# Sending the generated weights of a tile row to DRAM in two stages: four tap columns, then three

## The chip, the cores and the metric

The kernel runs on one core of a Trainium2 chip. The metric is device time in microseconds (us), given as the median of repeated runs. A profile of one execution stands beside it: its span is the time from the first to the last instruction.

## What is computed

Two layers over a batch of 32 images of 256 channels and 32 x 32 pixels. Each begins with a group normalization (`_gn`, 32 groups) and adds its result to its input.

```python
# layer 0: a 3x3 convolution in fp16 (values clamped), 256 -> 256 channels
x = x + _L0_conv_ref(_gn(x), L0_conv_weight, L0_conv_bias)
# layer 1: an involution, whose 7x7 kernels are generated at each pixel
y = jnp.einsum('oc,bchw->bohw', w1, x)                  # 256 -> 64
y = relu(y * scale + shift)                             # batch norm
w = jnp.einsum('oc,bchw->bohw', w2, y) + b2             # 64 -> 16 groups * 49 taps
w = w.reshape(b, G, K * K, H, W)
patches = ...                                           # 7x7 neighbourhood of each pixel
out = jnp.einsum('bgkhw,bgckhw->bgchw', w, patches)     # 16 groups of 16 channels
```

The x of the second part stands for the normalized input of layer 1. The weights w differ from pixel to pixel: 16 x 49 values at each of 1024 pixels of each image.

## The kernel before

**The work of one image.** `front(b)` does everything up to the generated features: group normalization, the convolution (line 332, tile `pc`), the second normalization, the features `y_sb`, and the transposed pixels. `weights(b, r0)` turns the features of four image rows (a chunk, WR = 4) into involution weights: TensorE multiplies into `pw` (line 410), and VectorE adds the bias and writes the result into `w_sb` (line 428).

`w_sb` is a ring of 24 image rows. The 7 tap columns dj lie in it by `divmod(dj, 2)`: the quotient picks one of four blocks of 32 partitions (one partition for each image column), the remainder e picks one of two planes. So even tap columns lie in plane e = 0 and odd ones in plane e = 1, and each is written by VectorE adds of its own.

**The way through DRAM.** The involution is done as matrix products against banded weights, and the layout needed for that is made by writing to DRAM and reading back:

- `scatter(b, k)` (line 477) writes the weights of tile row k (8 image rows, 4 tile rows an image) from `w_sb` to the DRAM tensor `wd`: one DMA of 160 KB for each of the 7 tap columns, all issued by SyncE (called SP in the profile).
- `load_bands(b, k)` (line 490) reads the tile row from `wd` into one of three band buffers: 16 DMAs of 70.2 KB, of which 14 are issued by GpSimd (POOL) and two by SyncE. All seven tap columns have to be in `wd` by then.
- `sums(b, m)` (line 515) multiplies pixels and bands on TensorE into `acc`, half a tile row at a time. `add_windows(b, m)` (line 531) adds `acc` to the image on VectorE.
- `store(b, k)` (line 536) writes half an image to the output and `load_x` (line 105) loads an image as two halves. Both are issued by SyncE, at 512 KB for each DMA.

**The order.** The order of instructions on each engine is written out by hand: a loop over steps n, 16 to an image. `due(n, lag)` says which image and which step i of that image a kind of work belongs to in step n. An engine executes its own instructions in this order and waits only where data or a buffer requires it, so a step is a place in each engine's queue and not a time. Within one step the order is: `front`, `sums`, `add_windows`, `store`, `weights`, `scatter`, `load_x`, `load_bands`.

With LEAD = 18, a chunk of weights is made in each even step. The scatter of a tile row is in the step after the last chunk that it needs. Counted modulo 16, the scatters of tile rows 0, 1, 2 and 3 fall into steps 3, 7, 11 and 13. The loads of bands fall into steps 3 (tile row 3 of the image before), 7 (tile row 0), 11 (tile row 1) and 15 (tile row 2). The stores fall into steps 12 (first half) and 15 (second half), and the load of an image into step 1. The bands of a tile row are loaded nine steps before its sums.

Of the kernel before, what the change touches and what calls it, by code (L numbers as in the profile page):

```python
# [14 lines left out]
B, C, H, W = 32, 256, 32, 32  # L15
# [5 lines left out]
K1, PAD1 = 7, 3  # L21
# [18 lines left out]
TR = RG * XR  # L40
SIDES = 2
JC = W // SIDES
K = H // TR
# [17 lines left out]
WR = 4  # L61
# [6 lines left out]
LEAD = 18  # L68
# [3 lines left out]
def tile_quant_conv_then_involution(  # L72
# [29 lines left out]
    def load_x(b):  # L102
        xt = xpool.tile([P, CH, N], F32, tag="x", name=f"x_{b}")
        for h in range(CH):
            nc.sync.dma_start(xt[:, h], x[b, h * P : (h + 1) * P])
        return xt
# [91 lines left out]
    def quantize_weights():  # L198

        for kh in range(CH):  # L200
            nc.vector.tensor_scalar(wq[:, kh], staged[kh], F16_MAX, -F16_MAX, ALU.min, ALU.max)
            nc.gpsimd.memset(bands[kh], 0.0)
        nc.gpsimd.memset(w_sb, 0.0)
# [198 lines left out]
    def weights(b, r0):  # L402

        pws = [ps_w.tile([P, 2, 2, SW], F32, tag=f"pw{i}", name=f"pw{i}") for i in range(2)]
        for r in range(2):
            for t in range(T):
                for i in range(2):
                    half = slice(i * CR, (i + 1) * CR)
                    dj = slice(2 * t, min(2 * t + 2, K1))
                    nc.tensor.matmul(  # L410
                        pws[i][t * TW : (t + 1) * TW, r, : dj.stop - dj.start],
                        y_sb[b % 2][half, (r0 // 2 + r) * W : (r0 // 2 + r + 1) * W],
                        w2_sb[half, dj],
                        start=True,
                        stop=True,
                    )
        for i in range(2):
            for e in range(2):
                p = P if e == 0 else (K1 // 2) * TW
                for r, rows, d0, d1, at in ring_pieces(b, r0 + 2 * i):  # L420

                    to = w_sb[:p, e]
                    to = bass.AP(
                        tensor=to.tensor,
                        offset=to.offset + at * WB + K1 - 1 - d0,
                        ap=[to.ap[0], [WB, rows], [WB - 1, d1 - d0], [WIN, G]],
                    )
                    nc.vector.tensor_tensor(  # L428
                        to,
                        pws[i][:p, r : r + rows, e, d0 * G : d1 * G].rearrange("p r (d g) -> p r d g", g=G),  # L430
                        b2_sb[:p, e, d0 * G : d1 * G]
                        .unsqueeze(1)
                        .to_broadcast([p, rows, (d1 - d0) * G])
                        .rearrange("p r (d g) -> p r d g", g=G),
                        ALU.add,
                    )
# [26 lines left out]
                    d += 1  # L463
        return pieces

    def scatter(b, k):

        at = (b * H + k * TR) % RING
        for dj in range(K1):
            t, e = divmod(dj, 2)  # L470
            to = bass.AP(
                tensor=wd.tensor,
                offset=wd.offset + k * TR * ROW + dj * WPIX + (K1 - 1 - dj) * WB,
                ap=[[WPIX, TW], [ROW, TR], [1, WB]],
            )
            rows = w_sb[t * TW : (t + 1) * TW, e, at : at + TR]
            nc.sync.dma_start(to, rows.rearrange("p s g r -> p s (g r)"))  # L477

    def load_bands(b, k):

        band = bands[(b * K + k) % NBAND]
        for i in range(JC):
            j = i // 2 + i % 2 * JC // 2
            src = bass.AP(
                tensor=wd.tensor,
                offset=wd.offset + k * TR * ROW + (j + PAD1) * WPIX,
                ap=[[ROW - 1, TR], [JC * WPIX, SIDES], [1, WPIX]],
            )
            queue = nc.sync if i % SHARE == SHARE - 1 else nc.gpsimd
            queue.dma_start(band[j::JC, :, j * WB : j * WB + WPIX], src)  # L490
# [10 lines left out]
    def sums(b, m):  # L501

        k, d = divmod(m, SIDES)
        j0 = 0 if d else PAD1
        band = bands[(b * K + k) % NBAND][:, d]
        px = pixels[(b * K + k) % NPIX][:, d]
        for h in range(CH):
            for v in range(2):
                for g, at, top, f, l in windows(b, m):
                    p = slice(g * KP, (g + 1) * KP)  # L510
                    of = band[p, g * XR + j0 * WB : g * XR + (j0 + WINI) * WB]
                    of = of.rearrange("p (j g r) -> p j g r", g=G, r=WIN)
                    for t in range(T):
                        a = h * T + t
                        nc.tensor.matmul(  # L515
                            at[t * TW : (t + 1) * TW, h, :, f - top : l - top],
                            px[p, a, v * GC : v * GC + TW],
                            of[:, :, 2 * a + v, f - top : l - top],
                            start=(h, v) == (0, 0),
                            stop=(h, v) == (CH - 1, 1),  # L520
                        )

    def add_windows(b, m):

        d = m % SIDES
        to = x_tiles[b].rearrange("p h (r c) -> p h r c", c=W)
        j0 = d * (JC - PAD1)
        for g, at, top, f, l in windows(b, m):
            x_at = to[:, :, f:l, j0 : j0 + WINI]
            of = at.rearrange("p h j r -> p h r j")[:, :, f - top : l - top]  # L530
            nc.vector.tensor_tensor(x_at, of, x_at, ALU.add)  # L531

    def store(b, k):

        cols = slice(k * NT, (k + 1) * NT)
        nc.sync.dma_start(out[b].rearrange("(h p) n -> p h n", p=P)[:, :, cols], x_tiles[b][:, :, cols])
# [5 lines left out]
    def due(n, lag):  # L542

        b, i = divmod(n - lag, per)
        return (b, i) if 0 <= b < B else (None, None)

    with tc.manual_schedule():
        fronts = {}
        for n in range(FRONT, B * per + 2):
            b, i = due(n, FRONT)  # L550
            if i == 0:
                fronts[b] = front(b)
            later = list(fronts)
            for part in range(2):
                for b in list(later):
                    got = next(fronts[b], fronts)
                    if got is fronts:
                        fronts.pop(b)
                    if got is not LATER:
                        later.remove(b)  # L560
            if n == FRONT + CH:
                quantize_weights()
            b, i = due(n, 0)
            if b is not None and i % 2 == 0:
                sums(b, i // 2)
            b, i = due(n, 1)
            if b is not None and i % 2 == 0:
                add_windows(b, i // 2)
                if i // 2 == M - 1:
                    store(b, 1)  # L570
                    x_tiles.pop(b)

            b, i = due(n, 2)
            if b is not None and i == 2 * (M - 1 - SIDES):
                store(b, 0)
            b, i = due(n, -LEAD)
            if b is not None and i % 2 == 0:
                weights(b, i // 2 * WR)

            b, i = due(n, -LEAD + 1)  # L580
            if b is not None and i % 2 == 0:
                for k in range(K):
                    if i // 2 == min((k + 1) * TR // WR, H // WR - 1):
                        scatter(b, k)
            b, i = due(n, LOAD)
            if i == 0 and b > 0:
                x_tiles[b] = load_x(b)

            b, i = due(n, 3 - 4 * NBAND)
            if b is not None and i % 4 == 0:  # L590
                load_bands(b, i // 4)
# [37 lines left out]
```

## Time and profile before

| What | Value |
|---|---|
| median of 3 runs | 1401.32 us (1395.67 to 1407.39) |
| time of the profiled execution | 1399.26 us |
| its span | 1397.5 us |
| mean granted TensorE clock | 0.979 |
| TensorE busy | 1263.0 us (90%) |
| GpSimd busy | 1009.8 us (72%) |
| VectorE busy | 926.6 us (66%) |
| ScalarE busy | 727.9 us (52%) |
| bytes moved by DMA | 369.33 MB |

Busy time is the time in which an engine executes; register, semaphore and branch instructions do not count, nor does the issue of DMAs by SyncE. GpSimd's busy time here is mostly the issue of its 1792 band loads, 548 ns each. Names such as `wd<-w_sb` say what is written and what is read. A wait is put down to what the trace saw end last before it.

### The profile page before, as it was taken

How to read it: one execution, taken by the hardware profiler on the slowest of the kernel's cores; microseconds unless marked ns; L12 is line 12 of the kernel's file. 1: busy time of each engine (PE TensorE's matmuls, PEld its weight loads, DVE VectorE, ACT ScalarE, POOL GpSimd, SP SyncE). 2: the span in 40 equal slices, each digit the busy share in tenths (PEclk: the TensorE clock that was granted, in tenths of full speed). 3: DMA queues.
4: the chain of work that ended last, by engine and by line, in shares of the span. 5: the costliest groups of instructions: out<-in, count | busy, mean ns of one | idle time of the engine just before them, and what ended most of it. 6: DMA issues, size and time to landing. Idle time of an engine off the chain costs nothing.

```text
span 1397.5 us, 70073 instructions
## 1 busy us (share of the span) xinstructions
PE 1263.0 (90%) x29440; PEld 801.1 (57%) x29440; DVE 926.6 (66%) x3179; ACT 727.9 (52%) x1699; POOL 1009.8 (72%) x1818
## 2 busy tenths in 40 slices
PE   4899999999999999998998999999999999999765
PEld 2455565556656566565655565655555655556544
DVE  3567677666776667676776666776666776777552
ACT  5865556455655546565554556463556564553200
POOL 9067777777777777778777777767776767777785
PEclk9999999999999999999999999999999999999876
DMA  6099999999999999999999999999999999999996
GB/s 215 16 248 276 253 283 289 280 274 272 286 284 274 287 278 281 278 285 274 280 287 272 272 273 282 263 278 275 273 282 267 265 282 277 282 264 269 252 257 187
DMA packets 366232, 369.33 MB, mean 264 GB/s; under 512 B 78624, under 2 KB 308192, under 8 KB 365664
## 3 DMA queue, kind: packets, MB, share of 16 engines
q1 hardware_dynamic: 279904, 235.72, 57.3%
q0 software_dynamic: 86016, 129.14, 34.7%
q8 instruction: 234, 3.83, 1.2%
q14 instruction: 78, 0.64, 0.2%
HBM read 183.81 MB, written 180.74 MB: 261 GB/s over the span
## 4 chain that ended last, share of the span: by engine, by line
PE 49%; DMA 30%; issue 6%; POOL 5%; DVE 4%; SPq 3%; ACT 2%; POOLq 0%; DVEq 0%; ACTq 0%
DMA band<-wd 23%; PE pc L332 20%; PE acc L515 15%; PE pw L410 9%; DMA wd<-w_sb 6%; POOL band L490 5%; PE py L380 3%; SPq L477 3%; DVE w_sb L428 2%; PE pt L395 2%; ACT junk L219 1%; DVE x L531 1%; DMA band<-in_w 1%; DMA x<-in_x 0%; ACT xn L278 0%
## 5 line engine op out<-in xcount | busy, mean ns | idle before, releaser
L490 POOL DMA_DIRECT2D band<-wd x1792 | 977.9, 548 | 375.4 <-DMA band<-wd 239.4
L428 DVE TENSOR_TENSOR w_sb<-pw,b_sb 128x16 f32<-128x16 f32 (+9 forms) x1920 | 454.3, 349 | 374.7 <-PE pw L410 362.0
L332 PE MATMUL pc<-xq,wq 128*128 128x496 f16 (+3 forms) x2304 | 535.1, 378 | 28.1 <-ACT xq L278 21.3
L515 PE MATMUL acc<-band,pixels 64*32 64x190 f32 (+1 forms) x16384 | 419.1, 323 | 73.8 <-DMA band<-wd 32.3
L515 PEld LDWEIGHTS acc<-band,pixels 64*32 64x32 f32 x16384 | 297.5, 108 | 165.9 <-issue 99.1
L332 PEld LDWEIGHTS <-wq 128*128 128x128 f16 x2304 | 206.5, 98 | 323.5 <-issue 110.2
L410 PE MATMUL pw<-w_sb,y 64*32 64x224 f32 (+1 forms) x8192 | 297.8, 333 | 24.1 <-issue 23.1
L531 DVE TENSOR_TENSOR x<-acc,x 128x380 f32<-128x380 f32 (+1 forms) x512 | 261.6, 511 | 35.7 <-PE acc L515 26.8
L410 PEld LDWEIGHTS pw<-w_sb,y 64*32 64x32 f32 x8192 | 183.2, 106 | 58.4 <-issue 40.6
L399 ACT COPY pixels<-pt 128x512 f32<-128x512 f32 x128 | 73.6, 575 | 234.7 <-PE pt L395 234.7
L219 ACT ACTIVATE junk<-x 128x512 f16<-128x512 f32 (+1 forms) x192 | 146.4, 763 | 14.7 <-DVE x L348 7.4
L219 ACT ACTIVATE junk<-x,mean 128x1024 f16<-128x1024 f32 x128 | 147.1, 1149 | 4.3
L250 ACT ACTIVATE s<-back,eps 128x2 f32<-128x2 f32 x64 | 18.9, 296 | 200.3 <-DVE back L235 200.2
L278 ACT ACTIVATE xn<-x,off,rstd 128x512 f32<-128x512 f32 x128 | 96.1, 800 | 0.0
L346 DVE TENSOR_SCALAR q<-pc 128x512 f16<-128x512 f32 x128 | 87.2, 681 | 12.5 <-PE pc L332 12.3
L348 DVE SCALAR_TENSOR_TENSOR x<-q,bias_sb,x 128x512 f32<-128x512 f16 x128 | 92.1, 719 | 0.2
L395 PEld LDWEIGHTS pt<-ident,xn 128*128 128x128 f32 x512 | 63.6, 142 | 27.1 <-issue 2.5
L395 PE MATMUL pt<-ident,xn 128*128 128x128 f32 x512 | 77.8, 275 | 1.2 <-ACT pixels L399 1.2
L278 ACT ACTIVATE xq<-x,off,rstd 128x1024 f16<-128x1024 f32 x64 | 76.0, 1228 | 1.4 <-PE pc L332 1.3
L240 ACT ACTIVATE mean<-back 128x2 f32<-128x2 f32 x64 | 12.7, 198 | 119.2 <-DVE back L235 119.0
L380 PEld LDWEIGHTS py<-xn,w_sb 128*64 128x64 f32 x2048 | 62.7, 138 | 16.3 <-issue 9.1
L380 PE MATMUL py<-xn,w_sb 128*64 128x64 f32 x2048 | 67.5, 224 | 2.3 <-ACT xn L278 1.8
(40 smaller groups left out, 369.5 us busy)
## 6 DMA issues: line engine op xcount, KB each, us to landing
wd<-w_sb SPq DMA_DIRECT2D x896, 160.0 KB
band<-wd POOLq DMA_DIRECT2D x1792, 70.2 KB, 5.0
x<-in_x SPq DMA_DIRECT2D x64, 512.0 KB
out<-x SPq DMA_DIRECT2D x64, 512.0 KB
band<-wd SPq DMA_DIRECT2D x256, 70.2 KB
band<-in_w SPq DMA_DIRECT2D x2, 1152.0 KB
w_sb<-in_w SPq DMA_DIRECT2D x2, 196.0 KB
wd<-band SPq DMA_DIRECT2D x2, 180.0 KB
```

Source lines behind the costliest of these rows:

```text
L219: nc.scalar.activation(junk[:, n0:n1], src[:, h, n0:n1], func, bias=bias, accum_out=self.sums[:, i : i + 1])
L278: nc.scalar.activation(dst, src, AF.Identity, bias=self.off[:, one], scale=self.rstd[:, one])
L332: nc.tensor.matmul(pc.rearrange("p (r c) -> p r c", c=W)[:, r0 - nt * RT : r1 - nt * RT, c0:c1], wq[:, kh, k, mh * P : (mh + 1) * P], xq[: ...
L346: nc.vector.tensor_scalar(q, pc, F16_MAX, -F16_MAX, ALU.min, ALU.max)
L348: nc.vector.scalar_tensor_tensor(xt[:, mh, cols], q, bias_sb[:, mh : mh + 1], xt[:, mh, cols], ALU.add, ALU.add)
L380: nc.tensor.matmul(py[i * CR : (i + 1) * CR, cols], w1_sb[:, kh, :], px[:, r : r + 2], start=kh == 0, stop=kh == CH - 1,)
L395: nc.tensor.transpose(pt[:, i, h * P : (h + 1) * P], xn[:, h, (m + i) * P : (m + i + 1) * P], ident)
L410: nc.tensor.matmul(pws[i][t * TW : (t + 1) * TW, r, : dj.stop - dj.start], y_sb[b % 2][half, (r0 // 2 + r) * W : (r0 // 2 + r + 1) * W], w ...
L428: nc.vector.tensor_tensor(to, pws[i][:p, r : r + rows, e, d0 * G : d1 * G].rearrange("p r (d g) -> p r d g", g=G), b2_sb[:p, e, d0 * G : d ...
L490: queue.dma_start(band[j::JC, :, j * WB : j * WB + WPIX], src)
L515: nc.tensor.matmul(at[t * TW : (t + 1) * TW, h, :, f - top : l - top], px[p, a, v * GC : v * GC + TW], of[:, :, 2 * a + v, f - top : l - top],
L531: nc.vector.tensor_tensor(x_at, of, x_at, ALU.add)
```

## The change

`scatter` gets an argument `part`. With part 0 it issues the tap columns 0, 2, 4 and 6, with part 1 the columns 1, 3 and 5. Part 0 stays in the step in which the whole scatter was. Part 1 is one step later, for each tile row. Within its step it stands where the scatter stands: after `store` and `weights`, ahead of `load_x` and `load_bands`.

```diff
-    def scatter(b, k):
+    def scatter(b, k, part):
 
         at = (b * H + k * TR) % RING
-        for dj in range(K1):
+        for dj in range(part, K1, 2):
             t, e = divmod(dj, 2)
...
-            b, i = due(n, -LEAD + 1)
-            if b is not None and i % 2 == 0:
-                for k in range(K):
-                    if i // 2 == min((k + 1) * TR // WR, H // WR - 1):
-                        scatter(b, k)
+            for part in range(2):
+                b, i = due(n, -LEAD + 1 + part)
+                if b is not None and i % 2 == 0:
+                    for k in range(K):
+                        if i // 2 == min((k + 1) * TR // WR, H // WR - 1):
+                            scatter(b, k, part)
             b, i = due(n, LOAD)
             if i == 0 and b > 0:
                 x_tiles[b] = load_x(b)
```

## The prediction

> **What bounds the kernel now.** I read the busy line and the slices first, then the waits, then the timelines of the two queues that issue the DMAs concerned.
>
> ```profile
> PE 1263.0 (90%) x29440; PEld 801.1 (57%) x29440; DVE 926.6 (66%) x3179; ACT 727.9 (52%) x1699; POOL 1009.8 (72%) x1818
> DMA  6099999999999999999999999999999999999996
> PE 49%; DMA 30%; issue 6%; POOL 5%; DVE 4%; SPq 3%; ACT 2%; POOLq 0%; DVEq 0%; ACTq 0%
> ```
>
> TensorE is busy in 90% of the span, and the DMA engines are above 90% in nearly every slice. The chain that ended last (third line) is half TensorE and about a third the transfers with the queues that issue them: DMA 30, POOL 5, SPq 3. So there are two near-equal bounds. Over 97 to 1350 us, the stretch without start and tail, the windows view gives TensorE 1166.4 of 1253 us, a DMA share of 0.97 and a clock of 0.99. The waits in that stretch:
>
> ```profile
> DVE w_sb L428 <- PE pw L410: 356.1, 225, 6.7
> POOL band L490 <- DMA band<-wd: 230.3, 284, 2.9
> ...
> POOL band L490 <- DMA wd<-w_sb: 19.1, 31, 2.7
> PE acc L515 <- DMA band<-wd: 18.7, 15, 2.6
> ...
> DVE w_sb L428 <- DMA wd<-w_sb: 6.6, 2, 4.2
> PE acc L515 <- DMA wd<-w_sb: 6.2, 6, 2.2
> ```
>
> Columns: total us, times, longest. GpSimd's band loads wait mainly for their own earlier landings (230.3), since eight may be outstanding: it issues in runs of about eight, 4.4 us each, then waits 1 to 2 us. TensorE loses only 18.7 + 6.2 = 25 us to transfers. The weights' way out to DRAM (wd<-w_sb) costs GpSimd at most 19.1 us and VectorE 6.6. SyncE and GpSimd around one tile row 0 (image 15):
>
> ```profile
> 673.54 1.32 SPq L105 DMA_DIRECT2D x<-in_x  x2
> 675.21 5.26 SPq L477 DMA_DIRECT2D wd<-w_sb  x7
> 680.86 1.64 SPq L490 DMA_DIRECT2D band<-wd  x2
> 682.86 5.97 SPq L477 DMA_DIRECT2D wd<-w_sb  x7
> ...
> 683.89 3.37 POOL L490 DMA_DIRECT2D band<-wd  x6
> 688.38 0.55 POOL L490 DMA_DIRECT2D band<-wd  x1 [1.13 <-DMA band<-wd]
> 689.14 3.32 POOL L490 DMA_DIRECT2D band<-wd  x6 [0.22 <-DMA wd<-w_sb]
> ```
>
> The seven taps take 5.3 us to issue, two band loads follow in 1.6 us, and GpSimd's first load of this tile row starts at 689.14. I read each landing from the semaphore updates: the last update of a DMA's semaphore before that semaphore's next DMA. Here the taps land from 681.9 to 686.8, so 689.14 stands 2.3 us after the last one.
>
> **What the skill says.** "DMA: Bandwidth & Descriptors", section "Queues, rings and completion order": every DMA engine takes turns between the queue rows, and consumes one row's ring in order. The trace agrees: the taps land in the order of issue, about 0.8 us apart, and an issue behind a 512 KB store or load lands late. The same page, "Anatomy of one DMA", prices a GpSimd DMA at about 2.0 us plus bytes/436 GB/s, which is an estimate of 2.2 us for 70.2 KB. The trace shows 2.4 at least but 5.0 in the median, so most of the landing time is sharing the engines. "Trainium Kernel Development and Optimization", "Key Constraints": DMAs of all issuers run on the same 16 engines. So moving transfers between places in a queue saves no bytes; the DMA share of 0.97 says the same.
>
> **The change, part by part.**
>
> *What moves.* All 896 taps stay, at 160 KB each. What SyncE executes is a fixed order in which it waits only for data; a step is no clock. The seven taps of a tile row were contiguous. Now taps 0, 2, 4, 6 go first and 1, 3, 5 go in the next step's place. A tile row is 10.2 us ((1368.6 - 66.3) / 127.5), a step a quarter of it, 2.6 us. Between the two stages now stand: for tile rows 0, 1 and 2, the two SyncE band loads of the tile row before (load_bands falls in the first stage's step); for row 2 also store(b, 0); for row 3 nothing. So the "stage" is worth 1.2 to 2.6 us of issue for the band loads and about 0.4 more for the store, not a full step.
>
> *Does anything hold the second stage longer?* The band loads wait for a buffer whose sums ran a step before. In the trace they start 0.1 to 1.6 us after row 0's last tap, so their data was ready. The store waits for add_windows of the step before it; behind row 2 of image 14 it issued at 660.0, right after the band loads. Each weights chunk on VectorE starts while the tile row before it is still in flight, so dependences are kept by region, and the second stage needs no later chunk. I cost extra waits at nothing, with 2 us as the upper end (the rest of a step).
>
> *When the last tap lands.* The place that tap 5 takes in the queue is today that of the second band load (rows 0, 1) or of the store (row 2). Bytes in the ring ahead of it are then the same, so I take their present landing. Against today's last tap, over images 2 to 29: row 0 +0.6 us, row 1 +1.5, row 2 +2.5 (512 KB are now ahead of it), row 3 about 0.
>
> *GpSimd.* Its first load of a tile row needs all seven taps. It starts, in the mean, 2.9, 4.4, 5.3 and 6.6 us after the last landing for rows 0 to 3; at least 0.8 of this is the pass through the waits. Subtracting 0.8 and the shifts above image by image leaves 3 of 28 rows 0 short by 1.6 us in total, one row 1 by nothing, and 3 rows 2 by 3.8: 5.4 us of new GpSimd waits. If all second stages land 1 us later still, the same sum is 19.6 us; 2 us later, 57.4. I take 8, because a 160 KB tap lands a little after a 70 KB load in the same place.
>
> *VectorE.* The ring of 24 rows in w_sb is overwritten three tile rows on. For row 0 the fifth chunk's adds come close: even taps (e = 0) have a margin of 1.3 us in the mean and 0.1 at the least, odd ones 2.4 and 1.0. The even taps now land earlier, a gain; the odd ones in the place of the band load fall short in 9 of 28 images by 5.2 us in total. VectorE already waits 356.1 us for TensorE ahead of just these adds, 1.6 us each time, and that hides it. I count 0; uncovered, it would be 5.
>
> *What reaches the end.* About half the chain runs through transfers and their issue (30 + 5 + 3 against 49 of TensorE), so half of 8 us: +4. Nothing offsets it: SyncE's two band loads go about 2.4 us earlier, but they land 6 to 9 us before GpSimd's last load, which decides when the sums start.
>
> Profiled execution: 1399.26 (span 1397.5, 1.8 around it) + 4 = 1403.3. The median of the runs shown, 1401.32, lies 2.1 above it, so 1405.
>
> **The rivals.**
>
> *Held for a whole step (slower).* The second stage waits for something not seen today: for example for the next chunk's adds, if they count as writers of its rows, or for add_windows ahead of the store. Price: 1.5 to 2 us more on each second stage, 35.2 to 57.4 us of GpSimd waits by the sum above; half reaches the end: +18 to +29, so 1424 (1401 + 23). It decides from a further 1.3 us of delay on, where the sum gives 27.6 us and its half is the 14 us of 1%. For it: row 0 has an average spare of only 1.5 us after the shift, and the sum is steep. Against: adds start while taps of other rows fly, and a GpSimd that slips gains margin for the rows that follow.
>
> *Smoother transfers (faster).* Bursts of seven taps become four and three, and GpSimd's loads land sooner. 23% of the chain, 321 us, is band landing. If the 5.0 us shrink by 5%, 16 us go: 1385. For it: landings range from 2.4 to 7.5 us. Against: total bytes and the share of 0.97 stay, and SyncE queues the same work back to back, so the engines see no gap where the burst was cut.
>
> *Nothing at all.* The stages stay nearly contiguous, the waits land where something waits anyway: 1401. It differs from my forecast by less than the runs can show, and I count it with it.
>
> **How the numbers follow.** About 1% is what a measurement of this kernel can tell from no change (the three runs spread over 0.8%). Forecast with "nothing at all" 0.72, held 0.20, smoother 0.08. The forecast's own range is 1397 to 1413; to leave out no more than 0.2 it goes to 1395 and 1418, which takes in the lighter half of the held case. Faster by over 1% 0.08, within 0.74, slower 0.18: a small part of the held case stays within 1%.
>
> **What would show it.** In the profile after: on SyncE four taps, two band loads, three taps for rows 0 and 1, with the store ahead of the three for row 2, and seven together for row 3; 896 taps and 369 MB unchanged; GpSimd's waits on wd<-w_sb up from 19.1 to 25 or 30 us; VectorE's waits on the same above 6.6; TensorE's on transfers near 25 to 30. Wrong would be a gap of over 1 us ahead of the three taps, GpSimd's waits on wd above 45 us, or a median landing of GpSimd's loads below 4.8 us.

## The result

The changed kernel takes 1390.96 us in the median of 20 runs (1378.52 to 1400.98). The kernel before, run beside it, takes 1395.55 us (1385.5 to 1407.39, 20 runs). The ratio is 0.9953 with a 95% interval of 0.9931 to 0.9974: about 6.6 us faster (3.6 to 9.6). It compares fast runs alone, without two runs of the change that lie over 1.5% above its fastest; the two medians by themselves are 4.6 us apart. The forecast was 1405 us, slower by 4. The three runs it started from lie 5.8 us above the later median of the same kernel. That shifts the forecast time, not its sign: a ratio of 1.003 is outside the interval.

The profiled execution took 1389.64 us, span 1387.9. Lines of its page:

```profile
PE 1250.5 (90%) x29440; PEld 798.5 (58%) x29440; DVE 934.7 (67%) x3179; ACT 727.6 (52%) x1699; POOL 1007.6 (73%) x1818
...
DMA  6079999999999998999999999999999999999995
...
PE 55%; DMA 25%; DVE 5%; issue 5%; POOL 4%; SPq 3%; ACT 3%; POOLq 0%; DVEq 0%; ACTq 0%
```

The work is the same and the DMA engines are as full as before. In the chain that ended last, transfers with their issue went from 38% (30 + 5 + 3) to 32% (25 + 4 + 3), TensorE from 49% to 55%. That step tells nothing about the cause: in two versions tried below that gain about the same as the change, this share is 43% (mixed_planes) and 18% (row01_staged). The waits between 97 and 1340 us, in the columns shown before:

```profile
DVE w_sb L428 <- PE pw L410: 334.6, 220, 5.9
...
POOL band L490 <- DMA band<-wd: 219.1, 299, 2.9
...
PE acc L515 <- DMA band<-wd: 25.6, 19, 3.1
...
POOL band L490 <- DMA wd<-w_sb: 18.1, 19, 3.6
...
DVE w_sb L428 <- DMA wd<-w_sb: 13.4, 13, 3.4
...
PE acc L515 <- DMA wd<-w_sb: 6.4, 3, 3.9
```

VectorE waits 13.4 us for the scatter where it waited 6.6, as the forecast expected. But GpSimd's wait for the scatter did not grow: 18.1 us after 19.1. TensorE's waits for transfers rose from 25 to 32 us (25.6 + 6.4), although the kernel became faster; its busy time fell from 1263.0 to 1250.5 us. So in this pair of profiles no wait of TensorE shows where the time went. SyncE's timeline in two stretches, around tile rows 2 and 3 of one image and rows 0 and 1 of the next:

```profile
661.28 1.22 SPq L490 DMA_DIRECT2D band<-wd  x2
662.54 0.44 SPq L536 DMA_DIRECT2D out<-x  x1
663.02 9.61 SPq L477 DMA_DIRECT2D wd<-w_sb  x10
...
680.36 2.74 SPq L477 DMA_DIRECT2D wd<-w_sb  x4
683.21 1.22 SPq L490 DMA_DIRECT2D band<-wd  x2
684.54 8.54 SPq L477 DMA_DIRECT2D wd<-w_sb  x7
693.25 1.82 SPq L490 DMA_DIRECT2D band<-wd  x2
```

The queue has the order that was forecast. The second stage of row 2 stands behind two band loads and the store, and runs on into row 3 (ten taps). Row 0's four taps are followed by two band loads; then come its last three taps and, without a gap, row 1's first four (seven together).

One profile of each kernel cannot show where 6.6 us went: runs of one kernel differ by more than that. The experiments below therefore rest on the ratios of 6 to 22 runs of each version, against the kernel before run beside it, and the profiles are used for waits that differ by tens of us. How far one profile's waits scatter can be seen from row01_staged below: it treats tile row 0 as the change does, and VectorE's waits on the scatter are 27.9 us there against 13.4.

### The profile page after: what moved, and what is told of

Its sections match the earlier page's. It is cut to its first block, busy times and chain, and to the rows that moved or that the text cites. A ratio compares the mean times of both kernels' runs of the same rounds, so it can differ in the third digit from the quotient of the medians.

```text
span 1387.9 us, 70012 instructions
## 1 busy us (share of the span) xinstructions
PE 1250.5 (90%) x29440; PEld 798.5 (58%) x29440; DVE 934.7 (67%) x3179; ACT 727.6 (52%) x1699; POOL 1007.6 (73%) x1818
## 2 busy tenths in 40 slices
DMA packets 366232, 369.33 MB, mean 266 GB/s; under 512 B 78624, under 2 KB 308192, under 8 KB 365664
## 4 chain that ended last, share of the span: by engine, by line
PE 55%; DMA 25%; DVE 5%; issue 5%; POOL 4%; SPq 3%; ACT 3%; POOLq 0%; DVEq 0%; ACTq 0%
PE pc L332 22%; PE acc L515 17%; DMA band<-wd 14%; PE pw L410 10%; DMA wd<-w_sb 8%; POOL band L490 4%; PE py L380 3%; DVE w_sb L428 3%; SPq L477 3%; PE pt L395 2%; DMA out<-x 1%; ACT junk L219 1%; DVE x L531 1%; DMA band<-in_w 1%; ACT xn L278 0%
## 5 line engine op out<-in xcount | busy, mean ns | idle before, releaser
L515 PE MATMUL acc<-band,pixels 64*32 64x190 f32 (+1 forms) x16384 | 411.6, 322 | 80.2 <-DMA band<-wd 44.6
L410 PE MATMUL pw<-w_sb,y 64*32 64x224 f32 (+1 forms) x8192 | 291.2, 332 | 15.1 <-issue 13.9
L240 ACT ACTIVATE mean<-back 128x2 f32<-128x2 f32 x64 | 12.7, 198 | 120.6 <-DVE back L235 120.6
```

The lines of the kernel that those rows point to most:

```text
L410: nc.tensor.matmul(pws[i][t * TW : (t + 1) * TW, r, : dj.stop - dj.start], y_sb[b % 2][half, (r0 // 2 + r) * W : (r0 // 2 + r + 1) * W], w ...
L515: nc.tensor.matmul(at[t * TW : (t + 1) * TW, h, :, f - top : l - top], px[p, a, v * GC : v * GC + TW], of[:, :, 2 * a + v, f - top : l - top],
```

## The experiments

Names for what the expectations test: theory S (the burst of seven is cut), theory Q (band loads and store get an earlier place on SyncE), theory P, later refined to W (the late taps hold VectorE, which has to overwrite plane 0 or 1 of the ring), and theory N (what counts is which blocks of 32 partitions the taps of one stage lie in).

**Order of taps alone, the split in natural order, everything late, and the store put back**

```diff
 order_only (on the kernel before)
-        for dj in range(K1):
+        for dj in (0, 2, 4, 6, 1, 3, 5):
 split_plain (on the change)
-        for dj in range(part, K1, 2):
+        for dj in ((0, 1, 2, 3), (4, 5, 6))[part]:
 all_late (on the kernel before)
-            b, i = due(n, -LEAD + 1)
+            b, i = due(n, -LEAD + 2)
 store_behind (on the change): the three lines of store(b, 0) stand below the scatter
```

> All seven taps stay in the first stage's place, but in the order 0, 2, 4, 6, 1, 3, 5. Theory S (the seven-tap burst is cut by band loads, so transfers share better): nothing changes, ratio to before 1.000, median landing of GpSimd's band loads at the 4.99 us of before. Theory P (planes: the even taps land first, so VectorE's adds into plane 0 and what hangs on them are free earlier): the whole gain, ratio 0.995. Theory Q (the band loads and the store get an earlier place on SyncE): 1.000.

Measured 1.0014 (0.9984 to 1.0044): the order alone gives nothing that can be measured.

> Two stages in the natural order of the taps: 0 to 3 in the first, 4 to 6 in the second. Theory S: the whole gain, ratio 0.995, landing of the band loads at about 4.92 us as after. Theory P: none, 1.000 or slower, since tap 6 of plane 0 lands late again and VectorE's first adds of the fifth chunk wait for it (its waits on wd<-w_sb at 13 us or more). Theory Q: 0.995.

Measured 1.0014 (0.9990 to 1.0038): two stages with taps 4, 5 and 6 late give nothing either. VectorE's waits in this run:

```profile
DVE w_sb L428 <- PE pw L410: 301.0, 198, 5.5
...
DVE w_sb L428 <- DMA wd<-w_sb: 52.1, 20, 5.4
...
POOL band L490 <- DMA wd<-w_sb: 24.7, 27, 2.8
...
PE pw L410 <- DVE w_sb L428: 5.2, 6, 3.2
```

VectorE waits 52.1 us for the scatter, not 13.4. Of this TensorE's wait for VectorE shows 5.2 us directly.

> The whole scatter, seven taps in natural order, goes one step later: behind the band loads and behind the store, in one burst again. Theory S: no gain, ratio 1.000 or above, because the burst is whole. Theory P: no gain, above 1.000. Theory Q: at least the gain of the two stages, 0.995 or less, unless the lateness of the taps (some 2 us for all seven) costs it back; then GpSimd's waits on wd<-w_sb rise well above 19 us.

Measured 1.1271 (1.1214 to 1.1328), far outside what any theory had. SyncE's waits and the engines' in this run:

```profile
SPq L490 <- DMA wd<-w_sb: 316.6, 109, 6.4
```

```profile
DVE w_sb L428 <- DMA wd<-w_sb: 269.1, 44, 9.3
...
POOL band L490 <- DMA wd<-w_sb: 185.1, 57, 6.2
PE pw L410 <- DVE w_sb L428: 111.9, 68, 5.4
```

SyncE itself stands still: the band loads of rows 0 and 1 now come right behind the same row's taps in its queue, with no taps of the next row between, so SyncE waits for those taps to land before it can go on. The last tap has the same place in the queue as in the change. What differs is that four more taps are behind the band loads. The granted clock was lower too, 0.931 against 0.979 before, and TensorE was busy for 1337.6 us against 1263.0. How much of the 12.7% goes with the lower clock, the runs do not separate.

> The change as it is, but store(b, 0) keeps its place behind the scatter: the second stage of tile row 2 is ahead of it. Theory S: most of the gain, 0.996, as three tile rows are still cut by band loads. Theory P: the whole gain, 0.995. Theory Q with the store as the part that counts: no gain, 1.000; with the band loads as that part: 0.995.

Measured 0.9974 (0.9950 to 0.9999). The middle value is a little over half of the gain, without the earlier store; the intervals do not separate this from the change.

**Which taps may be late**

```diff
 odd_first (on the change)
-        for dj in range(part, K1, 2):
+        for dj in range(1 - part, K1, 2):
 odd_first_swapped: the same, and in weights()
-            for e in range(2):
+            for e in (1, 0):
 mixed_planes, pairs_early, spread_tap6_last (each on the change)
-        for dj in range(part, K1, 2):
+        for dj in ((0, 3, 4, 6), (1, 2, 5))[part]:
+        for dj in ((0, 1, 4, 6), (2, 3, 5))[part]:
+        for dj in ((0, 3, 4, 1), (2, 5, 6))[part]:
```

> Two stages again, but taps 1, 3, 5 in the first and 0, 2, 4, 6 in the second. Theory W (the stages save about 10 us in transfers, and every us that VectorE waits for the late taps gives about 0.2 us back): plane 0, which VectorE writes first, is now the late one, so its waits on wd<-w_sb are at 40 to 60 us and the ratio is 1.001 to 1.005, like the split in natural order. Theory N (what counts is that the taps of a stage lie in different partition blocks, as in 0, 2, 4, 6 and in 1, 3, 5): 0.995 as after.

Measured 1.0043 (1.0025 to 1.0062); VectorE's waits on the scatter rose to 107.3 us. The direction is that of theory W, the wait twice its size.

> As odd_first, and VectorE writes plane 1 ahead of plane 0 in each pair of rows, so that the late plane is again the one it writes last. Theory W: VectorE's waits on wd<-w_sb fall well below those of odd_first, to 15 to 35 us (four taps are late here, not three), and the ratio lies 0.2 to 0.5% below that of odd_first, 0.996 to 1.000. Theory N: the same as odd_first, 0.995.

Measured 1.0039 (1.0018 to 1.0060), VectorE's waits 49.9 us. Half of the wait is gone and the time is not: a miss for theory W as I had put it. Two other waits may be why. With four taps late, SyncE's band loads wait 90.4 us for the scatter (28.0 in the change) and GpSimd 34.5 us (18.1).

> Two stages of taps 0, 3, 4, 6 and 1, 2, 5: within each stage every tap still lies in another block of 32 partitions, as in the change, but plane 0 now has tap 2 in the late stage. Theory W (late taps of plane 0 stop VectorE's first adds): VectorE's waits on wd<-w_sb at 35 to 55 us, the gain gone, 1.000 to 1.002 as in the split in natural order. Theory N (the partition blocks of a stage): 0.995.

Measured 0.9946 (0.9925 to 0.9967), VectorE's waits 25.0 us. Theory W missed here, in the wait (35 to 55 us) and in the ratio (1.000 to 1.002). One late tap of plane 0 costs less when it is not the last of all. Taken alone this looked like theory N, so the next two separate them.

> All rows staged, taps 0, 1, 4, 6 and then 2, 3, 5. Within a stage two taps share a block of 32 partitions, as in the split in natural order; but of plane 0 only tap 2 is late, and it is the first of the late ones. Theory W (VectorE's wait for late taps of plane 0 stalls TensorE two steps later): VectorE's waits on wd<-w_sb near 25 us, ratio 0.994 to 0.997. Theory N (taps of a stage must lie in different blocks): 1.000 to 1.002.

Measured 0.9954 (0.9927 to 0.9981), VectorE's waits 12.1 us.

> All rows staged, taps 0, 3, 4, 1 and then 2, 5, 6: the late ones in three different blocks, but tap 6 of plane 0 is the very last, as in the split in natural order. Theory W: VectorE's waits on wd<-w_sb at 45 to 60 us, TensorE's way from the sums of row 2's second half to those of row 3's first longer by 0.3 to 0.5 us an image, ratio 0.999 to 1.003. Theory N: 0.995.

Measured 0.9996 (0.9975 to 1.0017), VectorE's waits 37.3 us. The ratio is where theory W had it; the wait is smaller, and TensorE's way (6.66 us against 6.57 before) is not longer by the expected 0.3 to 0.5.

Theory N falls: sharing a partition block keeps the gain, and different blocks lose it. What fits all of them is that the gain goes when the last tap to land is one of plane 0. But the versions without the gain all have two or more late taps of plane 0, tap 6 among them. No run sends tap 6 last with all other taps of plane 0 early, so the place of the tap and the number of late ones are not separated. Over all versions in which every row has two stages:

| Second stage | VectorE's waits on the scatter, us | TensorE, half tile row 5 to 6, us | ratio |
|---|---|---|---|
| 1, 3, 5 (the change) | 13.4 | 6.51 | 0.9953 |
| 2, 3, 5 | 12.1 | 6.46 | 0.9954 |
| 1, 2, 5 | 25.0 | 6.55 | 0.9946 |
| 2, 5, 6 | 37.3 | 6.66 | 0.9996 |
| 4, 5, 6 | 52.1 | 7.04 | 1.0014 |
| 0, 2, 4, 6, planes swapped | 49.9 | 7.40 | 1.0039 |
| 0, 2, 4, 6 | 107.3 | 6.97 | 1.0043 |

The third column is read from the traces: from the first matmul of the sums of row 2's second half to that of row 3's first half, mean over images 2 to 29 (before: 6.57). The chunk whose adds overwrite row 0's ring rows (index 5, counted from 0; the texts above call it the fifth) comes one chunk ahead of this stretch. The weights of the next chunk lie in it, and on TensorE they wait for `pw` until VectorE has read it. The stretch is clearly longer, 6.97 to 7.40 us, in the three slowest versions of the table; the others lie within what the remaining versions scatter (6.5 to 6.8, all_late apart, with 7.8). So the path from VectorE's wait over this stretch to the time is seen in those three alone. With 2, 5 and 6 late the gain is lost and the stretch is not longer. The last tap of plane 0 need not be early: with 2 as a late one (mixed_planes, pairs_early) the ratio is no worse than the change's, and 0.9946 is the lowest of all, though not separable from 0.9953.

**Which tile row pays**

```diff
 row01_staged, row2_staged, row0_staged, row1_staged (on the change; rows is (0, 1), (2,), (0,) or (1,))
-                            scatter(b, k, part)
+                            if k in rows or part == 0:
+                                scatter(b, k, part if k in rows else None)
...
-        for dj in range(part, K1, 2):
+        for dj in (range(K1) if part is None else range(part, K1, 2)):
```

> Only tile rows 0 and 1 go in two stages; rows 2 and 3 go whole, in natural order, in the first place. So band loads cut two of four bursts and no store goes ahead of a tap. If the cut of the bursts by band loads is what pays: 0.996 to 0.997. If the earlier store of row 2 is: 1.000. VectorE's waits on wd<-w_sb at 5 to 15 us in both, from row 0.

Measured 0.9958 (0.9939 to 0.9978): the gain of the change, without row 2. VectorE's waits, 27.9 us, lie above the 5 to 15 expected.

> Only tile row 2 goes in two stages, so its second stage is behind two band loads and the store. If the cut of bursts by band loads is what pays: a third of it, 0.998. If the earlier store is: most of the gain, 0.996. VectorE's waits on wd<-w_sb at 5 to 10 us.

Measured 0.9984 (0.9963 to 1.0004): a part in the middle value, with an interval from most of the gain to none.

> Only tile row 0, whose taps follow the load of an image on SyncE, goes in two stages. If the cut of this burst carries the gain of rows 0 and 1 (ratio 0.9958 together): 0.996 to 0.997. If each cut counts the same: 0.998. If row 1's does: 1.000.

Measured 1.0001 (0.9977 to 1.0025): nothing that can be measured.

> Only tile row 1 goes in two stages. If row 0's cut carries the gain: 1.000. If each cut counts the same: 0.998. If row 1's does: 0.996.

Measured 0.9964 (0.9943 to 0.9985): most of it. So row 1, whose late taps stand behind the band loads of row 0, pays when it is staged alone. Row 0 alone does not, and for row 2 alone the interval leaves it open. The granted clock is no rival here: its mean over the counted runs is 0.980 in row1_staged and 0.980 in the kernel before, run beside it.

**What in row 1 pays**

```diff
 pause (on the kernel before; pause is a DRAM tensor that nothing reads)
-        for dj in range(K1):
+        for dj in (0, 2, 4, 6, 1, 3, 5):
+            if dj == 1 and k < 2:
+                for i in range(2):
+                    nc.sync.dma_start(pause[b, k, i], ident[:16, :16])
 row1_natural, row1_five_late (on row1_staged)
-        for dj in (range(K1) if part is None else range(part, K1, 2)):
+        for dj in (range(K1) if part is None else ((0, 1, 2, 3), (4, 5, 6))[part]):
+        for dj in (range(K1) if part is None else ((0, 2), (4, 6, 1, 3, 5))[part]):
```

> One stage, taps in the order 0, 2, 4, 6, 1, 3, 5; in tile rows 0 and 1, two DMAs of 1 KB that no other work uses stand between tap 6 and tap 1, and the band loads stay behind all seven. The burst is cut in time, by some 0.8 us of SyncE's issue, and no transfer moves ahead of another. If the cut itself pays: 0.997 to 0.998. If the band loads' place ahead of the three taps does: 1.000 to 1.002.

Measured 0.9994 (0.9974 to 1.0014). Cutting the burst in time, in rows 0 and 1, does not give what staging these rows gave (0.9958); a gain at the low end of what was expected (0.9974) is not excluded.

> Only tile row 1 staged, taps 0 to 3 and then 4 to 6. VectorE overwrites row 1's ring rows 8 us or more after its taps landed, so no tap of this row can hold it. Theory W: the same gain as with even taps first in row 1, 0.9964. Theory N: none, 1.000.

Measured 0.9982 (0.9954 to 1.0010): between the two expectations, and too wide to decide.

> Only tile row 1 staged, two taps first and five behind the two band loads. The last tap keeps its place in SyncE's queue. If the gain of row 1 comes from the band loads' earlier place in the queue: more of it than with three late taps, 0.993 to 0.996, unless SyncE then stands waiting for row 0's landing ahead of them (over 40 us of waits of the band loads on wd<-w_sb, and 0.998 or more). If it comes from the later last tap: 0.9964.

Measured 0.9975 (0.9955 to 0.9996), with SyncE's band loads waiting 56.3 us on the scatter. The wait that was named as the obstacle is there, and it undid what the run was to test: SyncE issues row 0's band loads 3.0 us after row 1's first tap in the mean (images 2 to 28), no sooner than with three late taps (3.1 in row1_staged; 5.8 before).

**Where the loss of the natural order sits, and the change without row 0**

```diff
 row0_natural (on row0_staged)
-        for dj in (range(K1) if part is None else range(part, K1, 2)):
+        for dj in (range(K1) if part is None else ((0, 1, 2, 3), (4, 5, 6))[part]):
 rows12_staged (as row01_staged, with rows (1, 2), and whole rows in the order 0, 2, 4, 6, 1, 3, 5)
```

> Only tile row 0 staged, taps 0 to 3 and then 4 to 6, so that the late taps of plane 0 (4 and 6) belong to the row whose ring rows VectorE overwrites soonest. Theory W with row 0 as its place: VectorE's waits on wd<-w_sb rise to 30 us or more, ratio 1.002 to 1.004, above the 1.0001 of row 0 staged with even taps first. If row 2 is where the late taps of plane 0 hurt: 1.000.

Measured 1.0029 (1.0005 to 1.0053), slower than before, though the interval overlaps that of row0_staged (0.9977 to 1.0025). Its waits:

```profile
DVE w_sb L428 <- PE pw L410: 306.0, 201, 5.9
...
DVE w_sb L428 <- DMA wd<-w_sb: 54.3, 14, 7.2
...
PE pw L410 <- DVE w_sb L428: 5.5, 8, 1.9
```

One row alone makes as much VectorE wait as the split of all rows had (54.3 us against 52.1). All of it stands at plane 0 of the chunk that overwrites row 0's ring rows, 14 times. But row 0 is the main place of W and not the only one: in split_plain 38.9 of the 52.1 us stand at this chunk and 13.2 at the chunk of index 1, which overwrites ring rows of row 2 of the image before.

> The change in tile rows 1 and 2 alone; rows 0 and 3 leave whole in the first place, even taps first. Row 0 staged alone gained nothing (1.0001) and carries VectorE's wait. If the gains of rows 1 (0.9964) and 2 (0.9984) add: 0.994 to 0.996, VectorE's waits on wd<-w_sb below 13 us: at least as good as the change. If row 0 adds something next to the others: 0.997.

Measured 0.9956 (0.9933 to 0.9979), VectorE's waits 17.4 us, above the 13 expected. The change without row 0's second stage is as fast as the change; not measurably faster than it.

## Why the prediction was wrong

**The queue's order: right.** Taps, band loads and store stand on SyncE as described, with the same 896 taps and 369.33 MB.

**The landing of the last tap: right in the main.** From the first tap's issue to the last tap's landing, mean over images 2 to 29, row 0 went from 11.5 to 12.2 us, row 1 from 10.3 to 11.1, row 2 from 10.1 to 12.8 and row 3 from 11.2 to 10.5. The shifts of +0.7, +0.8, +2.6 and -0.7 stand against +0.6, +1.5, +2.5 and 0.

**GpSimd's new waits, 8 us: wrong.** Its first load started 2.9, 4.4, 5.3 and 6.6 us after the last landing; now 2.3, 3.5, 2.6 and 7.2. The spare shrank about as worked out, but the waits stayed at 18.1 us (before 19.1), not 25 to 30. One profile is little evidence for 8 us, but the six versions that stage every row with three late taps have 11.2 to 24.8 us, 17.9 in the mean. So the term on which the whole +4 stood was not there. The sum counted images whose spare fell short on one trace's timings, with everything else held in place; that the kernel's other timings moved with it is the likely reason, and is not shown.

**"About half reaches the end": not usable.** The half was read from the chain of one profile. In the profiles here, all_late apart, the chain's share of transfers and their issue runs from 18% to 43%, and it does not follow the ratio.

**VectorE, counted as 0: in keeping with the runs.** The odd plane's adds at the chunk that overwrites row 0 wait 9.7 us in 11 images, against 5.2 us in 9 images worked out, and row0_staged, with a like wait (11.9 us), costs nothing that can be measured. What was not seen is how narrow the cover is: with taps 4 and 6 late in row 0 the wait is 54.3 us and the kernel loses 0.29%. That the even taps are the early ones stands in the prediction as a side remark; that no tap of plane 0 comes at the end goes with the gain in every version that stages all rows.

**Extra waits of the second stage, costed at nothing: partly wrong.** SyncE's band loads wait for the scatter 28.0 us now, 4.9 before:

```profile
SPq L490 <- DMA wd<-w_sb: 28.0, 38, 1.5
```

Of these 38 waits 34 stand at row 0's band loads. I looked at the band loads behind row 0 only, which belong to the row before. Those behind row 1's first four taps belong to row 0, whose last taps are barely issued. The upper end of 2 us was not reached (longest 1.5).

**"Nothing offsets it": this is the step that failed.** Staging row 1 alone gives 0.9964, rows 0 and 1 0.9958, rows 1 and 2 0.9956. I had argued that band loads which go 2.4 us earlier cannot help because GpSimd's last load lands 6 to 9 us after them. Row 1 staged alone is worth some 5 us (2 to 8), against a cost put at 4 us that did not come. The premise itself holds in the trace of the change: SyncE's two loads of a tile row go 2.3 us (row 0) and 2.9 us (row 1) earlier and land 8 to 11 us before GpSimd's last one. So it was right that the sums do not wait for these loads, and wrong that therefore nothing could be gained from moving them or the taps behind them.

**The rivals.** "Smoother transfers" had the sign, and about 40% of its size (6.6 of 16 us). Its landing time did fall, from 4.99 to 4.92 us in the median of GpSimd's loads, 1.4% where 5% was supposed. But its mechanism is not shown, and its sign may be luck: odd_first has 4.89 us and is slower, row1_staged has 5.00 and gains, and the pause, which cuts the bursts, gains nothing that can be measured. "Held for a whole step" did not happen here. all_late is not a test of it: there SyncE itself stands still, which the rival did not name. It does show that the whole scatter a step later costs far more (12.7%) than the 18 to 29 us priced.

**What stays open.** Why staging row 1 pays (the three versions of it: 0.9964, 0.9982, 0.9975, not separable). The order of taps (1.0014) does not account for it. Two things move together in it: row 0's band loads are issued earlier, and three taps of row 1 later. The pause comes near to moving one without the other. In it the last tap of row 1 is issued 5.7 us after the first, as in row1_staged (5.7; before 4.9), but row 0's band loads come 6.6 us after that first tap, not 3.1. It gave 0.9994. That speaks for the earlier band loads and against the later taps, but is no proof: the two intervals overlap, and the pause also delays the band loads. By what path the earlier band loads would save time, no run shows.

## What to carry to other kernels

Moving part of a burst behind other transfers in the same queue can pay even where the queue's engine is not the bound and no bytes are saved; but first find for each row which engine refills the buffer that the burst empties, and let those parts leave first that it overwrites first. A late stage was cheap here while the instructions behind it in the same queue waited little for it (28.0 us in the change), and dear when they waited long (316.6 us): all seven taps behind the same band loads, where the change has three, turned 0.5% gained into 12.7% lost. The chain that ended last is one path through one run; its shares are no factor for a forecast. And a wait sum worked out on one trace, with all else held still, is no forecast of a few us where runs differ by ten.

## What the runs showed that I had not expected

At the start, the copy of the convolution weights on VectorE differs between the two profiles (columns: shortest, median and longest in ns, then first and last start in us). Before:

```profile
L201 DVE TENSOR_SCALAR wq<-band x2: 1441/1601/1761, 8.5 to 12.1; 128x2304 f16<-128x2304 f32 x2
```

After, the same two instructions:

```profile
L201 DVE TENSOR_SCALAR wq<-band x2: 3727/5419/7111, 9.3 to 13.1; 128x2304 f16<-128x2304 f32 x2
```

```profile
13.05 5.97 POOL L202 MEMSET band<- 128x7048 f32 x1 [1.27 <-DVE wq L201]
```

In the second, the copy that starts at 13.1 us runs beside GpSimd's memset of a band buffer (13.05 to 19.02) and takes 7.1 us; before, the memsets began at 14.14, after both copies were done. The first sums start 7.2 us later in that profile (97.4 against 90.2). The change does not touch this part, and in the other 18 profiles the first sums start at 89.7 to 92.2 us. A second copy of over 4 us stands in two more of them, order_only and all_late, each beside this memset; all other copies take under 2. But in row01_staged the second copy overlaps the memset too and takes 1.7 us at most, while the memset takes 7.2 instead of 6.0. So lying beside each other is not enough as a cause of a slow copy, and no run here was made to test it.
